# Quarter-tile weights in layer 3 and a re-searched instruction order for a four-layer graph network

## The chip, the core and the metric

The kernel runs on one NeuronCore of a Trainium2 chip. The metric is the device time of one launch in microseconds; lower is better. The five engines of the core run their own instruction streams, each strictly in its own order, and wait for one another by semaphores: TensorE (PE: matrix products, with the weight loads PEld beside them), VectorE (DVE), ScalarE (ACT), GpSimd (POOL) and SyncE (SP, which here only issues DMAs).

## What is computed

There are 16 independent graphs, each with 1024 nodes of 256 features and a 1024 x 1024 adjacency matrix of zeros and ones. Four layers follow one another, each as "normalise, relu, graph layer, add to x":

```
h = relu(layernorm(x));  x = x + relu(h @ W_upd + mean over neighbours of (h @ W_msg) + bias)     # layer 0
h = relu(layernorm(x));  x = x + layernorm_per_head(relu(attention(h)) + h @ W)                   # layer 1: 4 heads of 64
h = relu(layernorm(x));  x = x + elu(attention(h))                                                # layer 2: 4 heads of 64
h = relu(layernorm(x));  x = x + attention(h)                                                     # layer 3: 1 head of 256
```

In the attentions the score of a pair of nodes is `leaky_relu(e_src[i] + e_dst[j])`, pairs without an edge are left out, a softmax is taken over j, and the result weighs the rows of `h @ W`.

## The kernel before

**The factored attention.** A softmax weight is `exp(leaky_relu(s + t))`. It is the larger of two products, each of a factor of i and a factor of j. After a factor of i has been divided out (a softmax allows it), the unnormalised weight of the pair is `max(r[i], tt[j]) * mask[j, i]`, and the remaining factor of j, `exp(t)`, is multiplied into the rows of `h @ W`. `terms` makes the factors: `es = exp((1 - slope) * s)` is transposed, goes to DRAM (`rd`, through SP) and comes back broadcast to all partitions (`r`, one DMA per head in `spread`); `tt = exp(-(1 - slope) * t)` stays in SBUF. `bounds` (lines 1050 to 1052) notes the extremes of t and s. At the end of the launch they are compared with `TERM_MAX`, and a general kernel, which is not entered with these inputs, would be taken if they were too large.

**The weights and the products.** `masked` (line 1083) is one VectorE `scalar_tensor_tensor`: for a block jb of 128 nodes it writes the weights for `hi - lo` nodes i into a tile `p` of 128 x 1024. In layers 1 and 2 it writes all 1024 columns, and the product of that block (line 1266, called "head product" below) is 16 small matrix products with 65 columns that go to alternate 64-wide halves of the array. Each of the 4 heads has 8 such blocks. In layer 3 one operation writes only 256 columns, and the product (line 1420) is two matrix products of 257 columns; there are 4 x 8 of them per graph. The tag `p` has six buffers of 128 x 1024, and each call of `masked` takes a new one, in layer 3 too. `terms` also takes one of them for `r4`, and so do the weight matrices at the start.

**The other work.** `norm_t` makes the layer norm (VectorE statistics, GpSimd's root, ScalarE's `hn`, TensorE's transposes at line 967, ScalarE's copy to `ht`). `project` (line 984) is `h @ W`. Layer 0 gathers with eight blocks of adjacency columns (`adjr`, three buffers, loaded on GpSimd's queue, lines 1143 and 1146); its masks for the later layers come from a second load of the adjacency (`nat`, on SP's queue), squared on ScalarE and transposed by DMA. The epilogues of the heads run on VectorE, ScalarE and GpSimd.

**What sets the order.** All instructions are recorded with `Plan.do`, each with its engine, a cost in microseconds written out by hand, what it reads and writes, and a priority: the position of its graph (`plan.pos`, which grows by the TensorE costs), plus a slack, plus the `RANK` of its stage and engine. `Plan.emit` then does list scheduling over all 16 graphs: at each step it takes the instruction that can start first by the costs and, where these are equal, the one of lowest priority value. The order in which it takes them is the order of the instructions on each engine; on the chip only this order and the semaphores remain. Graph b starts at position `b * SHIFT`, with `SHIFT` 38.75, and a gate holds graph b + 2 back until layer 3 of graph b has begun.

Of the kernel before, what the change touches and what calls it, by code (L numbers as in the profile page):

```python
# [25 lines left out]

SHIFT = 38.75

ENGINES = ("pe", "dve", "act", "pool", "sp")
RANK = {  # L30
    "load": (-255, -45, -146, -223, -161),
    "setup": (147, 44, -129, 45, 72),
    "norm0": (132, -159, -111, 18, -3),
    "split0": (-94, 119, -51, -165, -111),
    "mask": (77, 143, 41, 193, 218),
    "gather0": (241, -7, 71, 23, 10),
    "norm1": (-60, -62, -162, -146, -99),
    "project1": (20, 26, -5, 26, -6),
    "weights1": (-164, 7, -45, 57, -13),
    "heads1": (-192, -212, -213, -62, -111),  # L40
    "last1": (-26, -102, 9, -196, -80),
    "norm2": (-206, -157, 81, 6, -21),
    "project2": (79, -60, -360, 87, -40),
    "weights2": (94, -3, 153, -153, 12),
    "heads2": (-112, -33, -288, -105, -59),
    "last2": (-21, -230, -230, -36, -82),
    "norm3": (-477, -373, -518, -355, -261),
    "project3": (148, 162, -14, -78, 0),
    "weights3": (170, 143, 167, 44, 87),
    "last3": (43, -259, -75, -14, -59),  # L50
}
BUFS = {
    "x": 3, "ht": 2, "wide": 6, "mask": 3, "adjr": 3, "nat": 2, "sq": 2,
    "hn": 2, "r": 3, "p": 6, "o": 2, "t": 2, "y": 2, "rd": 4,
    "mv": 4, "st": 2, "rstd": 4, "shift": 4, "tt": 3, "es": 2, "dg": 2, "rden": 2, "sth": 1, "mh": 2, "rsh": 2,
    "acc": 2, "mm": 4,
# [15 lines left out]
class Plan:  # L72
# [8 lines left out]
    def __init__(self):  # L81
        self.ops, self.pos, self.gate, self.stage = [], 0.0, None, None

    def do(self, eng, cost, fn, r=(), w=(), lag=0.0, slack=0.0, kind="f", dma=0.0):

        k, deps = len(self.ops), set() if self.gate is None else {self.gate}
        for keys, writes in ((r, False), (w, True)):
            for key in keys:  # L90
                buf, part = key if isinstance(key, tuple) else (key, None)
                parts = [part, None] if part is not None else list(set(buf.last) | set(buf.readers) | {None})
                for q in parts:
                    if q in buf.last:
                        deps.add(buf.last[q])
                    if writes:
                        deps.update(buf.readers.get(q, ()))
                buf.users.append(k)
        for key in r:
            buf, part = key if isinstance(key, tuple) else (key, None)  # L100
            buf.readers.setdefault(part, []).append(k)
        for key in w:
            buf, part = key if isinstance(key, tuple) else (key, None)
            if part is None:
                buf.last, buf.readers = {}, {}
            buf.last[part] = k
            buf.readers[part] = []
        bufs = list(dict.fromkeys(key[0] if isinstance(key, tuple) else key for key in (*r, *w)))
        deps.discard(k)
        self.ops.append((eng, cost, lag, fn, deps, bufs, self.pos + slack + RANK[self.stage][ENGINES.index(eng)], kind, dma))  # L110
        if eng == "pe":
            self.pos += cost

    def emit(self):
# [6 lines left out]
        done, free, held = [None] * n, {}, {}  # L121
        kept, moved = "f", 0.0

# [5 lines left out]
        while ready:  # L129
            best = None  # L130
            for k in ready:
                eng, cost, lag, fn, deps, bufs, prio, kind, dma = self.ops[k]
                at = free.get(eng, 0.0)
# [7 lines left out]
                for buf in bufs:  # L141
                    if buf.t is None:
# [3 lines left out]
                        if len(ends) >= m:  # L146
# [3 lines left out]
                            at = max(at, ends[m - 1] + 0.1)  # L150
                if at is not None and (best is None or (at, prio, k) < best):
                    best = (at, prio, k)
            at, _, k = best
            eng, cost, lag, fn, deps, bufs, _, kind, dma = self.ops[k]
            for buf in bufs:
# [443 lines left out]
def tile_factored(  # L599
# [55 lines left out]
    deg = const.tile([P, B * NB], F32, name="f_deg")  # L655
    mx = const.tile([P, B * 9], F32, name="f_mx")
    rdn = const.tile([P, B * NB], F32, name="f_rdn")

# [249 lines left out]
    def norm_t(xs, by_block=False):  # L908
# [3 lines left out]
        for hf in range(2):  # L912
# [34 lines left out]
            for i2 in range(2):  # L947
# [20 lines left out]

                do("pe", 0.46, turn, r=[hn], w=[pt])
                i0 = (hf * nh + 2 * i2) * P  # L970
# [7 lines left out]
    def project(ps, ht, ib, w, lo, hi, k=0):  # L978


        def go():
            out = ps.t[:, : hi - lo] if hi - lo > D else ps.t[:, k, :]
            for c in range(KC):
                nc.tensor.matmul(  # L984
                    out,
                    ht.t[:, c, ib * P : (ib + 1) * P],
                    w.t[:, c, lo:hi],
                    start=(c == 0 and k == 0),
                    stop=(c == KC - 1),
                    skip_group_check=k > 0,  # L990
                )

        do("pe", 0.88, go, r=[(ht, ib // 2), w], w=[ps])

# [14 lines left out]
    def terms(wh, nh, slope, ecol, scol, k):  # L1009


        tt = buf(small, "tt", [P, NB, nh])
        r4 = buf(work, "p", [P, N])
        rd = buf(dram, "rd", [nh, N])

        def ed():
            return wh.t[:, :, ecol::E1][:, :, :nh] if nh > 1 else wh.t[:, :, ecol : ecol + 1]

        m = NB * nh
        es = buf(small, "es", [P, nh, NB])  # L1020
        do(
            "act",
            0.25,
            lambda: nc.scalar.activation(
                es.t, wh.t[:, :, scol : scol + nh].rearrange("p n h -> p h n"), AF.Exp, scale=1.0 - slope
            ),
            r=[(wh, ib) for ib in range(NB)],
            w=[es],
        )
# [3 lines left out]
            0.11,  # L1033
            lambda: nc.tensor.transpose(pt.t[:m, :P], es.t.rearrange("p h n -> p (h n)"), ident),
            r=[es],
            w=[pt],
# [10 lines left out]

        def bounds():
            es = wh.t[:, :, scol : scol + nh]
            nc.vector.tensor_reduce(mx[:, k : k + 1], ed(), AX.XY, ALU.max)  # L1050
            nc.vector.tensor_reduce(mx[:, k + 1 : k + 2], ed(), AX.XY, ALU.min, negate=True)
            nc.vector.tensor_reduce(mx[:, k + 2 : k + 3], es, AX.XY, ALU.max)

        do("dve", 0.4, bounds, r=[wh])

        def raise_t():
            nc.scalar.activation(tt.t, ed(), AF.Exp, scale=-(1.0 - slope))
            nc.scalar.activation(ed(), ed(), AF.Exp)

        do("act", 0.5, raise_t, w=[tt, wh])  # L1060

# [12 lines left out]

        return tt, spread

    def masked(r, tt, mask, jb, h, lo, hi):

        w = buf(work, "p", [P, N])
        do(  # L1080
            "dve",
            (hi - lo + 125) / 960.0,
            lambda: nc.vector.scalar_tensor_tensor(  # L1083
                w.t[:, : hi - lo], r.t[:, lo:hi], tt.t[:, jb, h : h + 1], mask.t[:, jb, lo:hi], op0=ALU.max, op1=ALU.mult
            ),
            r=[r, tt, mask],
            w=[w],
        )
        return w
# [143 lines left out]
    def heads(b, l, xs, mask, w, slope, epilogue, keep):  # L1233
# [19 lines left out]
        for h in range(H):  # L1253
# [5 lines left out]
            for jb in range(NB):  # L1259
# [13 lines left out]

                do("pe", 0.94, product, r=[p, xw], w=[ps], kind="c")
            plan.stage = f"heads{l}" if h + 1 < H else f"last{l}"
            epilogue(b, h, ps, wh, xs, 8.0 if h + 1 < H else 0.0)

# [18 lines left out]
    def epilogue1(b, h, ps, wh, xs, slack):  # L1296
# [44 lines left out]

        do("pool", 2.0, root, r=[mb], w=[rs], lag=0.9, slack=slack)
        do(
# [52 lines left out]
    def layer3(b, xs, mask):  # L1396
# [15 lines left out]
        for i2 in range(NB // 2):  # L1412
            plan.stage = "weights3"
            ps = buf(acc_p, "acc", [P, 2, 512])
            for jb in range(NB):
                w = masked(r, tt, mask, jb, 0, i2 * 2 * P, (i2 + 1) * 2 * P)

                def product(w=w, ps=ps, jb=jb):
                    for q in range(2):
                        nc.tensor.matmul(  # L1420
                            ps.t[:, q, : D + 1],
                            w.t[:, q * P : (q + 1) * P],
                            wh.t[:, jb, : D + 1],
                            start=(jb == 0),
                            stop=(jb == NB - 1),
                        )

                do("pe", 0.87, product, r=[w, (wh, jb)], w=[ps])
            k = b * NB + 2 * i2
# [11 lines left out]
            for q in range(2):  # L1441
                do(
                    "dve",
                    0.5,
                    lambda q=q, i2=i2, ps=ps, o=o, k=k: nc.vector.scalar_tensor_tensor(  # L1445
# [25 lines left out]
    for b in range(B):  # L1471
        plan.pos, plan.gate = b * SHIFT, gates.get(b)
        xs, adjr = load_x(b) if b else first, {k: load_adjr(b, k) for k in range(2)}
# [15 lines left out]
    nc.vector.tensor_reduce(tot, ps[:, : B * NB].rearrange("p (b n) -> p b n", n=NB), AX.X, ALU.add)  # L1489
    for k, (t, most) in enumerate(((tot, 0.0), (mx, TERM_MAX), (rdn, 1e30))):  # L1490
        nc.vector.tensor_scalar(t, t, most, None, op0=ALU.is_le)
        nc.vector.tensor_reduce(m[:, k : k + 1], t, AX.X, ALU.min)
# [58 lines left out]
```

## Time and profile before

| what | us |
|---|---|
| three runs, median (lowest, highest) | 2740.07 (2736.87, 2740.48) |
| the profiled execution | 2741.27 |
| its span, first to last instruction | 2739.4 |
| mean granted TensorE clock in it | 0.972 |
| VectorE, weights of 1024 columns (line 1083), 1024 of them | 1251.0 busy, 1276 ns each |
| VectorE, weights of 256 columns (line 1083), 512 of them | 222.4 busy, 477 ns each |
| TensorE, head products (line 1266), 1024 of 16 | 1064.6 busy |
| TensorE, layer-3 products (line 1420), 512 of 2 | 462.2 busy |

A row of the costliest groups has the line, the engine and the operation, the tiles as out<-in, the count, the busy time, the mean duration of one, and the idle time of the engine just before, with what ended it. Matrix products are pipelined, so the duration of one is longer than the distance from one start to the next, and each product of 32-bit numbers stands as two instructions in the trace (32 per head product, 4 per layer-3 product). "Granted clock" is the share of the full TensorE clock that was allowed in a stretch.

### The profile page before, as it was taken

What the parts mean: (1) busy time and instruction counts of PE and PEld (TensorE: products, weight loads), DVE (VectorE), ACT (ScalarE), POOL (GpSimd) and SP (SyncE); (2) the same over time, 40 slices, a digit from 0 to 9 for tenths busy, and PEclk for the clock granted to TensorE, in tenths of its full rate; (3) what the DMA queues carried; (4) which work ended last, traced back from release to release, by engine and by line L of the source; (5) the groups of instructions that cost most, each with busy time, mean ns of one, the idle gap of its engine ahead of it and who ended that gap; (6) DMA issues with size and microseconds to landing.
All of it is one profiled execution on the core that took longest, in us unless ns stands there. A gap on an engine that the chain in (4) does not pass through costs nothing. (4 is left out here: it accounts for less than half of the span.)

```text
span 2739.4 us, 92386 instructions
## 1 busy us (share of the span) xinstructions
PE 2547.4 (93%) x40667; PEld 2285.7 (83%) x40667; DVE 2357.3 (86%) x4790; ACT 1143.5 (42%) x2753; POOL 878.0 (32%) x907
## 2 busy tenths in 40 slices
PE   7867999999999999999999999999999999999786
PEld 6767798888888888889888889888888988888775
DVE  2699689898988989899898989989898898989884
ACT  4431625344353444525344452534435353453222
POOL 3332234324252332424224251422425133241210
PEclk9989999999999999999999999999999999999998
DMA  8724547356472745547255563735546263562121
GB/s 194 171 44 84 113 87 165 82 128 117 99 143 53 159 91 129 105 91 163 60 144 97 118 125 71 163 75 133 112 107 134 63 158 81 130 118 66 33 52 29
DMA packets 397318, 293.58 MB, mean 107 GB/s; under 512 B 179301, under 2 KB 345706, under 8 KB 396906
## 3 DMA queue, kind: packets, MB, share of 16 engines
q0 software_dynamic: 232992, 92.29, 24.8%
q1 hardware_dynamic: 160752, 193.05, 24.4%
q8 instruction: 321, 5.26, 0.8%
q10 hardware_dynamic: 3162, 2.24, 0.3%
q14 instruction: 91, 0.75, 0.1%
HBM read 228.21 MB, written 17.37 MB: 90 GB/s over the span
## 5 line engine op out<-in xcount | busy, mean ns | idle before, releaser
L1083 DVE SCALAR_TENSOR_TENSOR p<-r,tt,mask 128x1024 f32<-128x1024 f32 (+1 forms) x1536 | 1473.3, 1010 | 109.2 <-PE acc L1266 40.8
L1266 PE MATMUL acc<-wide,p 128*64 128x65 f32 x32768 | 1064.6, 227 | 135.7 <-DVE p L1083 129.3
L1266 PEld LDWEIGHTS acc<-wide,p 128*64 128x64 f32 x32768 | 1017.2, 141 | 204.0 <-issue 99.0
L984 PE MATMUL mm<-f_w,ht 128*128 128x264 f32 (+2 forms) x2048 | 477.0, 387 | 1.4 <-ACT ht L973 1.3
L1420 PE MATMUL acc<-wide,p 128*128 128x257 f32 x2048 | 462.2, 382 | 10.1 <-DVE p L1083 9.9
L1420 PEld LDWEIGHTS acc<-wide,p 128*128 128x128 f32 x2048 | 386.1, 191 | 68.1 <-issue 11.1
L984 PEld LDWEIGHTS mm<-f_w,ht 128*128 128x128 f32 x2048 | 384.6, 192 | 61.2 <-ACT ht L973 3.0
L954 ACT ACTIVATE hn<-x,shift,rstd 128x256 f32<-128x256 f32 x512 | 269.1, 591 | 257.5 <-DVE shift L941 157.1
L1356 ACT ACTIVATE t<-t,mh,rsh 128x64 f32<-128x64 f32 x512 | 176.7, 428 | 198.2 <-DVE mh L1346 174.3
L1143 PE MATMUL mm<-wide,adjr 128*128 128x258 f32 x1024 | 254.5, 289 | 0.0
L1146 PE MATMUL mm<-wide,adjr 128*128 128x256 f32 x1024 | 247.9, 282 | 0.0
L1003 ACT COPY wide<-mm 128x264 f32<-128x264 f32 (+1 forms) x384 | 141.3, 378 | 218.7 <-PE mm L984 216.5
L1216 POOL DMA_DIRECT2D x<-y x48 | 76.6, 1596 | 447.4 <-DVE y L1388 435.8
L934 POOL TENSOR_SCALAR rstd<-mv 128x4 f32<-128x4 f32 x128 | 60.7, 474 | 434.6 <-DVE mv L929 402.3
L1143 PEld LDWEIGHTS mm<-wide,adjr 128*128 128x128 f32 x1024 | 195.9, 191 | 1.7
L1146 PEld LDWEIGHTS mm<-wide,adjr 128*128 128x128 f32 x1024 | 194.2, 190 | 1.5
L922 DVE BATCH_NORM_STATS2 st<-x 128x6 f32<-128x256 f32 x512 | 183.2, 412 | 8.4 <-DMA x<-in_x_dram 5.6
L967 PE MATMUL mm<-f_ident,hn 128*128 128x128 f32 x1024 | 168.0, 300 | 20.2 <-ACT hn L954 17.2
L973 ACT COPY ht<-mm 128x512 f32<-128x512 f32 x256 | 137.8, 580 | 104.9 <-PE mm L967 103.9
L1157 POOL TENSOR_SCALAR dg<-f_deg 128x1 f32<-128x1 f32 x128 | 61.0, 476 | 359.7 <-ACT f_deg L1154 357.4
L967 PEld LDWEIGHTS mm<-f_ident,hn 128*128 128x128 f32 x1024 | 125.2, 151 | 50.4 <-ACT hn L954 35.5
L935 POOL TENSOR_TENSOR rstd<-rstd,f_mhalf 128x4 f32<-128x4 f32 x128 | 162.2, 1268 | 10.7
(103 smaller groups left out, 2179.3 us busy)
## 6 DMA issues: line engine op xcount, KB each, us to landing
r<-rd SPq DMA_DIRECT2D x144, 512.0 KB, 3.9
adjr<-in_adj_dram POOLq DMA_DIRECT2D x128, 512.0 KB, 4.7
nat<-in_adj_dram SPq DMA_DIRECT2D x128, 512.0 KB, 6.6
out_dram<-o SPq DMA_DIRECT2D x64, 256.0 KB, 2.8
x<-in_x_dram SPq DMA_DIRECT2D x31, 512.0 KB, 5.1
x<-t POOLq DMA_DIRECT2D x48, 256.0 KB, 5.5
x<-y POOLq DMA_DIRECT2D x48, 256.0 KB, 4.5
mask<-sq SPq DMA_TRANSPOSE x128, 4.7
```

What stands on the lines that cost most here:

```text
L922: lambda st=st, ib=ib, k=k: nc.vector.bn_stats(st.t[:, k, :], xs.t[:, ib, :]),
L935: nc.gpsimd.tensor_tensor(rstd.t, rstd.t, mhalf[:, :nh], op=ALU.pow)
L954: nc.scalar.activation(hn.t[:, k, :], xs.t[:, hf * nh + q, :], AF.Relu, bias=shift.t[:, q : q + 1], scale=rstd.t[:, q : q + 1],)
L967: nc.tensor.transpose(pt.t[:, k, c, :], hn.t[:, k, c * P : (c + 1) * P], ident)
L984: nc.tensor.matmul(out, ht.t[:, c, ib * P : (ib + 1) * P], w.t[:, c, lo:hi], start=(c == 0 and k == 0), stop=(c == KC - 1), skip_group_che ...
L1003: lambda ib=ib, ps=ps: nc.scalar.copy(wh.t[:, ib, :cols], ps.t[:, :cols]),
L1083: lambda: nc.vector.scalar_tensor_tensor(w.t[:, : hi - lo], r.t[:, lo:hi], tt.t[:, jb, h : h + 1], mask.t[:, jb, lo:hi], op0=ALU.max, op1= ...
L1143: nc.tensor.matmul(ps.t[:, : D + 2], a.t[:, ib, :], hi.t[:, ib, : D + 2], start=(ib == 0), stop=False)
L1146: nc.tensor.matmul(ps.t[:, :D], a.t[:, ib, :], lo.t[:, ib, :D], start=False, stop=(ib == NB - 1))
L1266: nc.tensor.matmul(ps.t[c : c + 64, g, q * E1 : (q + 1) * E1], p.t[:, i2 * 64 : (i2 + 1) * 64], xw.t[:, jb, h * E1 : (h + 1) * E1], start= ...
L1356: nc.scalar.activation(t.t[:, ib, :], t.t[:, ib, :], AF.Identity, bias=mb.t[:, 3, ib : ib + 1], scale=rs.t[:, ib : ib + 1],)
L1420: nc.tensor.matmul(ps.t[:, q, : D + 1], w.t[:, q * P : (q + 1) * P], wh.t[:, jb, : D + 1], start=(jb == 0), stop=(jb == NB - 1),)
```

## The change

Layer 3's weights share a tile: four calls of `masked` fill the four quarters of one `p`, and each product reads its own quarter. `r4` moves out of `p` into a tag of its own with one buffer of 128 x 128. `tt` and `es` become the two halves of one tile `et`, and the check of the terms' size reads the exponentials instead of their arguments (two reductions instead of three, against limits `f_lim` which six memsets write at the start).

`Plan` gets three rules. Operations that carry a `row` (all calls of `masked` within a graph) must follow each other in the order in which they were recorded. An operation whose start lies within `HOLD` of the earliest on the same engine may go before it if its priority value is lower. A count of weights made and not yet used (`stock`) could favour weights below `LOW`; with `FIRST = 0` it does nothing. `SHIFT` becomes 193.25, each graph gets an offset `START`, the `RANK` table and the slacks of the epilogues get new numbers, and some costs change (transposes 0.46 to 0.5, projections 0.88 to 0.89, head products 0.94 to 0.955, layer-3 products 0.87 to 0.875, GpSimd's head root 2.0 to 2.6).

```diff
-SHIFT = 38.75
+SHIFT = 193.25
+LOW, FIRST = 5, 0
+HOLD = (0.1, 0.2, 0.1, 0.0, 0.0)
+START = (83, 357, 209, 320, 312, 341, 221, 275, 166, 245, 168, 116, 90, 156, 43, -288)
 RANK = {
...
-    "weights2": (94, -3, 153, -153, 12),
-    "heads2": (-112, -33, -288, -105, -59),
+    "weights2": (-26, 73, 114, -256, 21),
+    "heads2": (-318, -725, -739, -720, -508),
...
-    "mv": 4, "st": 2, "rstd": 4, "shift": 4, "tt": 3, "es": 2, "dg": 2, "rden": 2, "sth": 1, "mh": 2, "rsh": 2,
+    "mv": 4, "st": 2, "rstd": 4, "shift": 4, "et": 3, "r4": 1, "dg": 2, "rden": 2, "sth": 1, "mh": 2, "rsh": 2,
...
+        if row is not None:
+            if row in self.rows:
+                deps.add(self.rows[row])
+            self.rows[row] = k
...
-                if at is not None and (best is None or (at, prio, k) < best):
-                    best = (at, prio, k)
-            at, _, k = best
...
+                if at is not None:
+                    could.append((at, prio, k))
+                    if best is None or could[-1] < best:
+                        best = could[-1]
+            at, prio, k = best
+            until = at + HOLD[ENGINES.index(self.ops[k][0])]
+            for a, p, q in could:
+                if self.ops[q][0] == self.ops[k][0] and a <= until and p < prio:
+                    at, prio, k = a, p, q
...
-        r4 = buf(work, "p", [P, N])
+        r4 = buf(small, "r4", [P, P])
...
-            nc.vector.tensor_reduce(mx[:, k : k + 1], ed(), AX.XY, ALU.max)
-            nc.vector.tensor_reduce(mx[:, k + 1 : k + 2], ed(), AX.XY, ALU.min, negate=True)
-            nc.vector.tensor_reduce(mx[:, k + 2 : k + 3], es, AX.XY, ALU.max)
...
+            nc.vector.tensor_reduce(mx[:, k : k + 2], et.t.rearrange("p s h n -> p s (h n)"), AX.X, ALU.max)
+            nc.vector.tensor_reduce(mx[:, k + 2 : k + 3], ed(), AX.XY, ALU.max)
...
-    def masked(r, tt, mask, jb, h, lo, hi):
+    def masked(r, tt, mask, jb, h, lo, hi, w=None, q=0):
...
-        w = buf(work, "p", [P, N])
+        w = w or buf(work, "p", [P, N])
+        c = q * (hi - lo)
...
-                w.t[:, : hi - lo], r.t[:, lo:hi], tt.t[:, jb, h : h + 1], mask.t[:, jb, lo:hi], op0=ALU.max, op1=ALU.mult
+                w.t[:, c : c + hi - lo],
+                r.t[:, lo:hi],
+                tt.t[:, 1, h, jb : jb + 1],
+                mask.t[:, jb, lo:hi],
+                op0=ALU.max,
+                op1=ALU.mult,
             ),
-            r=[r, tt, mask],
-            w=[w],
+            r=[r, (tt, 1), mask],
+            w=[(w, q)],
+            row="weights",
+            stock=1,
...
-                w = masked(r, tt, mask, jb, 0, i2 * 2 * P, (i2 + 1) * 2 * P)
-
-                def product(w=w, ps=ps, jb=jb):
-                    for q in range(2):
+                q = jb % 4
+                w = masked(r, tt, mask, jb, 0, i2 * 2 * P, (i2 + 1) * 2 * P, w if q else None, q)
+
+                def product(w=w, ps=ps, jb=jb, q=q):
+                    for k in range(2):
+                        c = (2 * q + k) * P
...
-        plan.pos, plan.gate = b * SHIFT, gates.get(b)
+        plan.rows = {}
+        plan.pos, plan.gate = b * SHIFT + START[b], gates.get(b)
```

## The prediction

> **What bounds the kernel now.** I read the page first, then the busy time by 90 us windows, the waits, the timeline around one wait, and the order in which the two built programs hold their instructions.
>
> ```profile
> PE 2547.4 (93%) x40667; PEld 2285.7 (83%) x40667; DVE 2357.3 (86%) x4790; ACT 1143.5 (42%) x2753; POOL 878.0 (32%) x907
> ...
> PE   7867999999999999999999999999999999999786
> ```
>
> ```profile
> 180.00:270.00 90.00, 69.57 (x1661) 64.06 (x1659) 87.66 (x146) 24.60 (x62) 25.60 (x16) 0.87 0.34 70
> ...
> 810.00:900.00 90.00, 89.33 (x1324) 79.50 (x1324) 79.58 (x145) 29.85 (x73) 22.54 (x25) 1.00 0.33 66
> 900.00:990.00 90.00, 84.46 (x1310) 75.15 (x1309) 83.11 (x205) 51.09 (x124) 44.10 (x46) 0.98 0.72 153
> ...
> 2610.00:2700.00 90.00, 71.06 (x1180) 60.71 (x1179) 58.53 (x93) 26.09 (x60) 7.26 (x7) 0.92 0.21 46
> ```
>
> The columns are busy PE, PEld, DVE, ACT and POOL, granted clock, DMA share and GB/s. TensorE sets the time, with VectorE close behind it, and the loss has three places: the first 290 us, a repeated dip in the middle, and the last 220 us.
>
> ```profile
> PE acc L1266 <- DVE p L1083: 129.3, 56, 8.5
> ...
> DVE p L1083 <- PE acc L1420: 35.3, 79, 4.9
> ```
>
> TensorE waits for VectorE's weights 129.3 us in all, and elsewhere VectorE waits, 79 times, for layer 3's products to give a buffer back. The two are one event, seen around 900 us on TensorE and then on VectorE:
>
> ```profile
> 895.81 5.37 PE L1420 MATMUL acc<-wide,p 128*128 128x257 f32 x24
> 905.31 1.67 PE L1266 MATMUL acc<-wide,p 128*64 128x65 f32 x32 [4.14 <-DVE p L1083]
> ```
>
> ```profile
> 896.66 1.66 DVE L1083 SCALAR_TENSOR_TENSOR p<-r,tt,mask 128x256 f32<-128x256 f32 x4
> 898.24 0.68 DVE L1388 SCALAR_TENSOR_TENSOR y<-y,t 128x512 f32<-128x512 f32 x1
> 898.96 0.69 DVE L1227 TENSOR_TENSOR x<-x,y 128x512 f32<-128x512 f32 x1
> 899.68 1.40 DVE L922 BATCH_NORM_STATS2 st<-x 128x6 f32<-128x256 f32 x4
> ...
> 903.89 2.47 DVE L1083 SCALAR_TENSOR_TENSOR p<-r,tt,mask 128x1024 f32<-128x1024 f32 x2
> ```
>
> Each layer-3 weight takes a whole one of the six buffers `p`, though it fills a quarter. So TensorE has six products in hand (24 instructions, 5.37 us), while VectorE is away from weights for 5.6 us (898.24 to 903.89) and then needs 1.2 us more. The wait comes in every graph. What follows it is in the windows of TensorE alone:
>
> ```profile
> 901.20:905.30 4.10, 0.00 (x0) 1.00 0.42 124
> 905.70:909.10 3.40, 3.40 (x41) 0.51 1.20 292
> ```
>
> After 4.1 us idle, 3.4 us run at half clock (6.8 us in other graphs).
>
> **The ledger of before,** against this execution's own span of 2739.4 us (2741.3 with what lies around it; the median of the runs is 2740.1). Work at the start-to-start distance of undisturbed rows: 1024 head products at 0.944 us, 512 layer-3 products at 0.868, 512 projections at 0.876, 128 gathers at 1.90, 256 groups of four transposes at 0.436, 64 updates at 2.17, and 23 us of small ones: 2377 us. The order holds 176 excursions out of head products into other work and back. Eight in a row take 7.69 us and nine 8.62, so 0.93 each and 0.25 for the way in and out; start-to-start it is 0.12 and 0.09. With the gathers' changes this is 46 us. Total 2423; the other 316 is loss. In the middle a graph takes 162.3 us (eleven recurrences of this wait, 581.1 to 2366.4) for 151.3 us of work and changes. Its loss of 11.0 is 5.2 waits (4.13, 0.58, 0.51), 2.6 half clock, and 3.2 small delays. By 290 us the loss is about 94, and 71 come in the tail.
>
> **Part 1: quarter tiles and the order, middle.** Six buffers now hold 24 layer-3 weights, 21 us of products instead of 5. VectorE's work is unchanged (512 operations of 128x256, 0.396 us start to start). I laid VectorE's instructions between a released buffer and the next needed weight against TensorE's work between the same two points, with these row durations. In before this gives a deficit of 4.2 us per graph (trace: 4.1 and 0.6 over the same stretch); in after the worst stretch of a graph is 1.3 to 2.1. I take 2.3, and 0.5 for ScalarE as now: the waits fall from 5.2 to 2.8, a gain of 2.4. If the cover fails (another chain, say `rsh` on GpSimd, holds VectorE), it is 5.2 again.
>
> A rule bears on what the shorter waits do to the clock. The row: 4.1 us idle, then 3.4 to 6.8 at half rate; between 2644 and 2669 us six waits of 0.6 to 0.9 cost no clock. The Trainium skill ("TensorE: Matmul & The Clock Gate", Part 1) says that the clock halves after at least one idle window of about 3.4 us. By the rule all 2.6 us per graph go; by the row I keep 0.6 for bad alignment: gain 2.0.
>
> **Part 2: more changes of kind.** The new order breaks the products up to keep VectorE abreast: runs of 8 head products become runs of 2 to 5, and the excursions go from 176 to 326. At 0.21, with the gathers' changes, that is 83 us instead of 46: +37, of which 2.4 per graph. The skill speaks against exactly this: "TensorEngine Tiling (Array Packing)", Key Properties, says that a change of tiling mode drains the array, and head products write 64-wide tiles among 128-wide work. It names no price; at the 0.25 of the rows above, modelled ends included, the extra would be about 44. I take 37, because the start-to-start distance is what the next instruction sees. Middle: -2.4 -2.0 +2.4 = -2.0 per graph, over 13.4 graphs **-27**.
>
> **Part 3: the start.** In before the first products stand behind 83 us of TensorE work, in which two graphs are mixed, and start at 111.5. With DMA 94% busy in the first 90 us, graph 1's loads are ahead of what graph 0 needs. In after, 67 us stand ahead, all eight of graph 0's gathers come before any of graph 1's, and its adjacency loads come first on both SP's and GpSimd's queue. Until its last gather graph 0 needs some 11.8 MB (two graphs' `x`, the weight matrices, the adjacency for `adjr` and `nat`), 60 us at the 196 GB/s of the first window. I put the eighth gather at 64 us (75.5 now) and the first product at 95. From there VectorE sets the pace: before its last large start wait VectorE has 200 us of work ahead in before, 155 in after for 166 of TensorE's. With 79 us idle instead of 87, TensorE is 68 us late instead of 94: **-26**. Bounds: nothing, if the DMA is no earlier; -40, if the weights start at 80.
>
> **Part 4: the tail.** In before TensorE ends with graph 15 alone:
>
> ```profile
> 2681.88 3.14 PE L967 MATMUL mm<-f_ident,hn 128*128 128x128 f32 x12 [7.80 <-ACT hn L954]
> ...
> 2701.28 29.59 PE L1420 MATMUL acc<-wide,p 128*128 128x257 f32 x128 [6.27 <-DVE p L1083]
> ```
>
> These two waits and the half clock that follows (10.2 and 6.8 us at 0.5) make 22 us. In after, eight of graph 14's layer-3 products stand in the first gap, and twelve more around graph 15's `es` transpose, ahead of its own first product: 7 and 10 us of work for gaps of 7.8 and 6.3. The earlier tail, where VectorE is short (deficit 29 in either order), stays. **-22.** Changes of kind in the start and tail: **+5**.
>
> **Part 5: edits with one answer.** `bounds` reads exponentials in two reductions instead of three: VectorE -0.1 us, 48 times, under TensorE's work. It is due later; now VectorE stands 111 us behind ScalarE there, and in after some 3 us per graph remain, in time that VectorE has. `r4` leaves the six `p` and gets one buffer, wanted three times in 160 us: nothing. Six memsets on GpSimd before the first load: +0.2 us. `START`, `HOLD`, the per-graph order of weights and the costs act only through the order.
>
> **Sum:** 2740 - 27 - 26 - 22 + 5 = **2670 us**.
>
> **Rivals.** (a) *The changes of kind are paid and the waits come back.* My deficits follow VectorE and TensorE only. The new order puts `shift` and `mh` a few quarter weights behind GpSimd's roots (0.9 and 2.3 us), and VectorE queues behind them. If that brings over 5 us of waits per graph, with their half clock, the middle loses 2.4 x 13.4 = 32 and start and tail gain nothing: 2740 + 37 = **2777**. The point is a wait of about 5 us per graph. Against it: VectorE has 15 us to spare per graph (162.3 against 2357.3/16). 12%. (b) *Only the middle works:* the start is held by DMA and the tail by its chain: 2740 - 27 + 5, about **2718**. For it: DMA at 0.94. 18%. (c) *The small delays of 3.2 us go with the waits,* since they sit in the windows of low clock: 2.4 x 13.4 further, **2638**. 17%. (d) *The same time:* gains and changes of kind cancel, 4%.
>
> **Numbers.** My forecast 49%, the rest as above. From 2632 to 2728 leaves about 2 in 10 outside. A measurement of this kernel can't tell less than 0.2% (5.5 us) from no change: faster 84%, same 4%, slower 12%.
>
> **What would show it.** Right: no 4 us wait at a layer's start in the middle, hardly any half-clock window between 400 and 2400 us, a graph in about 160 us, the first product near 95 us, PE's last gap before layer 3 filled. Wrong: a wait of 4 us per graph elsewhere, a graph over 162 us, the first product still after 105 us.

## The result, and the profile after

The changed kernel takes **2757.4 us** (median of four runs, 2752.0 to 2759.2) against 2740.3 for the kernel before, measured beside it (2736.9 to 2742.7): a ratio of 1.006, 95% interval 1.0042 to 1.0078. It is slower by 0.6%, where 2670 was forecast. Its profiled execution took 2752.0 us, with a span of 2750.1 and a mean granted clock of 0.984 (before: 2739.4 and 0.972).

First the page of the changed kernel: busy time and instructions by engine, and TensorE's busy tenths in 40 slices.

```profile
PE 2587.8 (94%) x40667; PEld 2262.6 (82%) x40667; DVE 2350.8 (85%) x4742; ACT 1143.3 (42%) x2753; POOL 852.9 (31%) x913
...
PE   7878999999999999999999999999999999998788
```

The same 40667 TensorE instructions are busy for 40 us more (2547.4 before), although the clock is higher. Against this TensorE stands idle for 162 us instead of 192. The waits of TensorE (total us, times, longest) show that the wait of before has gone from its place:

```profile
PE acc L1297 <- DVE p L1107: 49.8, 51, 5.4
PE acc L1297 <- DVE o L1478: 21.5, 6, 6.2
PE mm L992 <- ACT hn L979: 18.3, 4, 13.2
PE acc L1297 <- DVE t L1317: 17.0, 19, 2.4
```

The waits for weights fell from 129.3 to 49.8 us. Two of these rows are new, those of `o` and of `t`. In both TensorE has a weight in hand, and waits for VectorE's epilogue to read out one of the two `acc` buffers. One such event, in TensorE's timeline (start, length, instruction, idle time before it and its releaser) and then in VectorE's:

```profile
1545.19 9.80 PE L1453 MATMUL acc<-wide,p 128*128 128x257 f32 x44
1559.15 3.74 PE L1297 MATMUL acc<-wide,p 128*64 128x65 f32 x64 [4.16 <-DVE o L1478]
```

```profile
1552.14 1.28 DVE L1107 SCALAR_TENSOR_TENSOR p<-r,et,mask 128x1024 f32<-128x1024 f32 x1 [4.57 <-issue]
...
1554.78 1.41 DVE L947 BATCH_NORM_STATS2 st<-x 128x6 f32<-128x256 f32 x4
...
1558.12 0.88 DVE L1478 SCALAR_TENSOR_TENSOR o<-acc,f_rdn,x 128x256 f32<-128x256 f32 x2
```

The quarter tiles do what they were forecast to do: eleven layer-3 products run in a row. But then VectorE, which stood 4.57 us for a reason that the profile doesn't name, and has a weight, an epilogue and two rounds of statistics ahead of `o` in its queue, gives `acc` back some 4 us late.

**The ledger.** Up to the start of the last TensorE instruction, the time is split as in the prediction: waits (idle time before instructions), half clock (half the length of the windows with a granted clock of 0.5), work (instructions times the start-to-start distance of undisturbed ones), and the rest, which is what changes of kind cost and stalls too short to show as idle time. The experiments are added for later reading; "excursions" are read from the order of the instructions. Idle time within half-clock windows (34 us before, 20 in the changed kernel) counts in full as a wait and by half as half clock, so the rest comes out too small; the last column has it with this time counted once.

| kernel | waits | half clock | work | rest | end | excursions | rest, idle once |
|---|---|---|---|---|---|---|---|
| before | 186 | 78 | 2380 | 89 | 2733 | 176 | 106 |
| changed | 156 | 46 | 2380 | 162 | 2744 | 326 | 171 |
| before, cheap weights | 140 | 68 | 2380 | 53 | 2640 | 176 | 66 |
| changed, cheap weights | 117 | 31 | 2380 | 127 | 2656 | 326 | 133 |
| before, wide head products | 121 | 290 | 3243 | -10 | 3644 | 176 | 8 |
| changed, wide head products | 64 | 159 | 3243 | 10 | 3476 | 326 | 19 |
| quarter tiles only | 327 | 119 | 2380 | 94 | 2920 | 145 | 132 |
| price raised in the list | 330 | 121 | 2380 | 120 | 2951 | 119 | 149 |
| changed, reordered | 119 | 22 | 2380 | 145 | 2666 | 282 | 150 |
| before, reordered | 193 | 71 | 2380 | 83 | 2727 | 196 | 99 |
| changed, reordered, old price | 121 | 35 | 2380 | 143 | 2679 | 351 | 152 |
| changed, reordered longer | 124 | 29 | 2380 | 134 | 2667 | 263 | 138 |

The changed kernel saves 30 us of waits and 32 of half clock and loses 73 in the rest: 11 us, the difference of the spans. I had charged 37 for the last and 107 as gain for the first two. So of the 81 us between forecast (-70) and ledger (+11), 45 are gains that fell short and 36 are the rest.

Where the rest comes from can be read in the two traces. I took each TensorE instruction's distance from the one before it, less idle time, half clock and the undisturbed distance. The first instruction after a change out of or back to head products and the two behind it are late by 43 us in all before, and by 100 in the changed kernel: 57 of the 66 us of the last column. But the rest is no count of excursions alone: with the price raised in the list it is 149 us at 119 excursions, and there the short stalls within runs are some 90 us, for some 40 in the changed kernel.

### The profile page after: what moved, and what is told of

Same layout as the page of the kernel before. It is cut to its first block, busy times and chain, and to the rows that moved or that the text cites. A ratio compares the mean times of both kernels' runs of the same rounds, so it can differ in the third digit from the quotient of the medians.

```text
span 2750.1 us, 92338 instructions
## 1 busy us (share of the span) xinstructions
PE 2587.8 (94%) x40667; PEld 2262.6 (82%) x40667; DVE 2350.8 (85%) x4742; ACT 1143.3 (42%) x2753; POOL 852.9 (31%) x913
## 4 chain that ended last, share of the span: by engine, by line
PE 58%; DVE 26%; DMA 6%; issue 5%; POOL 3%; ACT 2%; SPq 0%; ACTq 0%; DVEq 0%; POOLq 0%
PE acc L1297 21%; DVE p L1107 13%; PE mm L1009 11%; PE acc L1453 10%; PE mm L1213 4%; PE mm L1174 4%; PE mm L1177 4%; DMA r<-rd 3%; DVE st L947 2%; PE mm L992 2%; DMA mask<-sq 2%; DVE t L1317 2%; DVE sth L1360 2%; POOL rstd L960 1%; DVE t L1349 1%
## 5 line engine op out<-in xcount | busy, mean ns | idle before, releaser
L1107 DVE SCALAR_TENSOR_TENSOR p<-r,et,mask 128x1024 f32<-128x1024 f32 (+1 forms) x1536 | 1466.1, 1010 | 77.3 <-DMA r<-rd 35.7
L1297 PE MATMUL acc<-wide,p 128*64 128x65 f32 x32768 | 1087.9, 226 | 108.1 <-DVE p L1107 49.8
L1009 PE MATMUL mm<-f_w,ht 128*128 128x264 f32 (+2 forms) x2048 | 500.7, 391 | 1.6 <-ACT ht L998 1.6
L1453 PE MATMUL acc<-wide,p 128*128 128x257 f32 x2048 | 485.5, 384 | 5.9 <-DVE p L1107 2.0
L1009 PEld LDWEIGHTS mm<-f_w,ht 128*128 128x128 f32 x2048 | 376.1, 191 | 65.6 <-ACT ht L998 8.1
L1453 PEld LDWEIGHTS acc<-wide,p 128*128 128x128 f32 x2048 | 379.0, 190 | 60.2 <-issue 7.5
L992 PE MATMUL mm<-f_ident,hn 128*128 128x128 f32 x1024 | 157.2, 287 | 19.7 <-ACT hn L979 18.3
L904 POOL DMA_DIRECT2D adjr<-in_adj_dram x128 | 128.2, 1072 | 94.0 <-PE mm L1177 90.8
L992 PEld LDWEIGHTS mm<-f_ident,hn 128*128 128x128 f32 x1024 | 117.8, 144 | 46.5 <-ACT hn L979 26.2
```

What stands on the lines that cost most here:

```text
L992: nc.tensor.transpose(pt.t[:, k, c, :], hn.t[:, k, c * P : (c + 1) * P], ident)
L1009: nc.tensor.matmul(out, ht.t[:, c, ib * P : (ib + 1) * P], w.t[:, c, lo:hi], start=(c == 0 and k == 0), stop=(c == KC - 1), skip_group_che ...
L1107: lambda: nc.vector.scalar_tensor_tensor(w.t[:, c : c + hi - lo], r.t[:, lo:hi], tt.t[:, 1, h, jb : jb + 1], mask.t[:, jb, lo:hi], op0=ALU ...
L1297: nc.tensor.matmul(ps.t[c : c + 64, g, q * E1 : (q + 1) * E1], p.t[:, i2 * 64 : (i2 + 1) * 64], xw.t[:, jb, h * E1 : (h + 1) * E1], start= ...
L1453: nc.tensor.matmul(ps.t[:, k, : D + 1], w.t[:, c : c + P], wh.t[:, jb, : D + 1], start=(jb == 0), stop=(jb == NB - 1),)
```

## The experiments

Theory: an excursion out of the head products and back costs about 0.37 us, not 0.21, because the next instruction but one is late too. Rivals: the price is right and VectorE's waits, in its own queue order, eat the gain; or the quarter tiles are good and the new order spoils them.

**1. The price alone.** Stages of TensorE products on operands in SBUF, with equal work and a different number of excursions:

```diff
+    stages = (
+        (head, acc, 8, project, mm, 4, 1), (head, acc, 2, project, mm, 1, 4),
+        (head, acc, 8, last, ac2, 4, 1), (head, acc, 2, last, ac2, 1, 4),
+        (wide, acc, 8, project, mm, 4, 1), (wide, acc, 2, project, mm, 1, 4),
+    )
```

> Nothing of the stack is computed: six stages of TensorE products alone, on operands that are in SBUF. Stages 1 and 2 hold the same 80 head products and 40 projections, with 10 excursions out of the head products and with 40; stages 3 and 4 the same with 40 layer-3 products instead of projections; stages 5 and 6 as 1 and 2, with the head product as eight matmuls 128 columns wide instead of sixteen of 64. Theory (an excursion costs 0.37 us: 0.12 to leave, 0.10 at the second instruction of the entered run, 0.09 to come back, 0.05 at the third head matmul): stage 2 is 30 x 0.37 = 11 us longer than stage 1, stage 4 as much longer than stage 3, stage 6 within 1 us of stage 5. Rival (my prediction's 0.21 us, the rest being waits for VectorE): 6.3 us and 6.3 us. Rival (the cost is of any change of operand, not of the tile's width): stage 6 is also 6 to 11 us longer than stage 5.

TensorE's timeline in the first stage, then in the second:

```profile
29.71 7.69 PE L51 MATMUL acc<-wh,p 128*64 128x65 f32 x256
37.32 3.83 PE L72 MATMUL mm<-w,ht 128*128 128x264 f32 x16
41.08 7.69 PE L51 MATMUL acc<-wh,p 128*64 128x65 f32 x256
...
201.38 2.09 PE L51 MATMUL acc<-wh,p 128*64 128x65 f32 x64
203.40 1.16 PE L72 MATMUL mm<-w,ht 128*128 128x264 f32 x4
204.48 2.09 PE L51 MATMUL acc<-wh,p 128*64 128x65 f32 x64
```

Starts are compared, not lengths. Eight head products and four projections take 41.08 - 29.71 = 11.37 us; two and one take 3.10, and four times that is 12.41. Three more excursions cost 1.04 us, **0.346 each**. With layer-3 products the medians are 11.28 and 3.08: 0.347. With wide head products they are 17.853 and 4.463: 0.000. The theory holds. Another operand or another output alone costs nothing here; the cost belongs to the change between 64-wide and 128-wide tiles (whether to the width or to leaving the alternation of the two halves, these stages don't part).

**2. No reading of the exponentials.** The two reductions of `bounds` are left out (their target `mx` is set to zero once at the start):

```diff
-            nc.vector.tensor_reduce(mx[:, k : k + 2], et.t.rearrange("p s h n -> p s (h n)"), AX.X, ALU.max)
-            nc.vector.tensor_reduce(mx[:, k + 2 : k + 3], ed(), AX.XY, ALU.max)
+            pass
```

> Changed kernel without the two reductions over ScalarE's exponentials (48 x 2 VectorE instructions; the check value of the bounds is not computed), same order of everything else. Rival (VectorE's wait for ScalarE there, 6.4 us per graph, ahead of weights in its queue, makes TensorE's new waits): 30 us or more faster than the changed kernel, about 2725. Theory (the price of the excursions carries the loss; this wait lies in time that VectorE has): within 10 us of the changed kernel, 2747 to 2757.

Measured: 2755.7 us, ratio to before 1.0056 (1.0043 to 1.0069), so the same as the changed kernel. In the changed kernel VectorE waits 99.8 us for those exponentials. Here, in VectorE's waits and then in TensorE's:

```profile
DVE wide L1278 <- ACT wide L1075: 124.2, 18, 13.9
```

```profile
PE acc L1297 <- DVE p L1107: 48.3, 52, 5.4
PE acc L1297 <- DVE o L1478: 20.5, 6, 6.2
```

VectorE's wait is taken over by the next instruction that needs ScalarE: its row was 21.4 us, which with the 99.8 makes 121. TensorE's waits stay. So the two reductions cost nothing where they stand. What VectorE's wait for ScalarE itself costs, this run can't tell, because the wait did not go away; it is 6.4 us per graph in the middle (70.2 us over eleven graphs) where the prediction had 3.

**3. Wide head products,** in the changed kernel and in the one before, same order. The head product writes the same values with eight matrix products of 128 columns:

```diff
-                    for i2 in range(2 * NB):
-                        g, q = divmod(i2 // 2, 4)
-                        c = i2 % 2 * 64
+                    for i2 in range(NB):
+                        g, q = divmod(i2, 4)
...
-                            ps.t[c : c + 64, g, q * E1 : (q + 1) * E1],
-                            p.t[:, i2 * 64 : (i2 + 1) * 64],
+                            ps.t[:, g, q * E1 : (q + 1) * E1],
+                            p.t[:, i2 * P : (i2 + 1) * P],
```

> Changed kernel, same order, the head product as eight matmuls of 128 columns instead of sixteen of 64, so that no excursion changes the tile's width. If a wide product takes the same 0.94 us: theory (0.37 us per excursion, 326 of them) takes up to 120 us out of TensorE's work, of which VectorE (2357 us busy) lets some half show: 2650 to 2700. Rival (0.21 us): at most 68 us out, 2690 to 2730. Rival (stalls behind VectorE's order are what the change lost by): 2740 or more.

> Kernel before, same order, with the same wide head products. Theory (0.37 us, 176 excursions): at most 65 us less, 2685 to 2715, and slower than the wide changed kernel by 20 us or more, since with the price gone the quarter tiles' gain stands alone. Rival (0.21 us): at most 37 less, 2705 to 2730. Rival (the order's stalls carry the loss): the wide changed kernel is again no faster than this one.

Measured: 3504 and 3650 us, ratios to before 1.280 and 1.330. The forecasts of both totals rested on a wide product that takes the same 0.94 us, and it takes 1.79 (first experiment), so the totals answer nothing. The ledger does. The rest now differs by 20 us between the two orders instead of by 73 (by 10 instead of 66 with idle time counted once): without changes of width, 53 to 56 us of the difference are gone, which is 150 excursions at 0.35 to 0.37. What stays I put down to the other changes of kind, those into and out of the gathers and the products that prepare them (the "fp32r split"). The new order has 107 more of them (185 for 78), but no run tries them alone. And the changed kernel is now the faster one, by 168 us in the profiled executions (146 by the medians): 57 less in waits and 131 in half clock, 20 more in the rest. Most of this is half clock, which wide products keep for long stretches (last section), so its size says little of quarter tiles. TensorE's wait for weights in the kernel before with wide products, then in the changed one, where it comes second to 17.6 us for `hn`:

```profile
PE acc L1265 <- DVE p L1083: 81.7, 21, 6.9
```

```profile
PE acc L1296 <- DVE p L1107: 12.1, 6, 4.2
```

**4. Cheap weights,** in both kernels, same orders:

```diff
-                w.t[:, : hi - lo], r.t[:, lo:hi], tt.t[:, jb, h : h + 1], mask.t[:, jb, lo:hi], op0=ALU.max, op1=ALU.mult
+            lambda: nc.vector.tensor_copy(w.t[:, : hi - lo], r.t[:, lo:hi]),
```

> Kernel before, same order on every engine, each attention weight made by a plain copy of r instead of the maximum times the mask (the mask and the exponentials are not applied), so that VectorE's largest operation takes about half as long and its work falls from 2357 to some 1700 us. TensorE's 192 us of waits and most of its half clock then have no cause but the start, the tail and other engines: all theories expect 2500 to 2600 here. It is the base for the next run.

> Changed kernel, same order, the same cheap weights. Theory (the order's 150 more excursions cost 0.35 us each whatever VectorE does): slower than the kernel before with cheap weights by 30 to 55 us, the 52 us of excursions less what the earlier start of graph 0 saves. Rival (the loss is new waits behind VectorE's order, which now has slack): no slower, or faster by up to 20 us.

Measured: 2647.3 and 2669.8 us (ratios 0.9647 and 0.9735). VectorE falls to 1730 us of work in the first and 1723 in the second, and the new order is still 22 us slower. The base did not come down to the 2500 to 2600 us that I expected: TensorE waits 140 us in it, for 186 before, and most of that is still for weights, though they are cheap:

```profile
PE acc L1264 <- DVE p L1083: 86.0, 25, 7.8
```

So two thirds of the 129.3 us stay when a weight of 1024 columns takes 713 ns for 1276. In the pages of the two (busy time by engine):

```profile
PE 2500.8 (94%) x40667; PEld 2272.3 (86%) x40667; DVE 1729.8 (65%) x4790; ACT 1141.8 (43%) x2753; POOL 802.8 (30%) x907
```

```profile
PE 2538.5 (95%) x40667; PEld 2239.4 (84%) x40667; DVE 1722.6 (65%) x4742; ACT 1137.9 (43%) x2753; POOL 784.5 (29%) x913
```

The rival falls: with a VectorE that has slack the rest differs by 74 us, as with the full weights (67 and 66 with idle time counted once). The result lies below the 30 to 55 that the theory gave, since I left out that the quarter tiles still save 22 us of waits and 37 of half clock here.

**5. Quarter tiles alone, and the price told to the list.** The first is the kernel before with the four quarters in one `p` and nothing else; the second changes one line of the changed kernel:

```diff
-    EMPTY = {"cf": 0.12, "cr": 0.12, "fc": 0.09, "fr": 0.09, "rc": 0.09, "rf": 0.19}
+    EMPTY = {"cf": 0.23, "cr": 0.23, "fc": 0.14, "fr": 0.09, "rc": 0.14, "rf": 0.19}
```

> Kernel before with layer 3's weights in quarter tiles and nothing else (old ranks, old costs, no order of the weights, no hold). By its instruction order it has 145 excursions (176 before, 326 in the changed kernel), and VectorE's work between a freed buffer and the next needed weight exceeds TensorE's between the same points by 197 us in all (128 before, 73 changed). Theory (both excursions and deficits count, each at its measured price): 31 x 0.35 = 11 us less and up to 69 us more wait: 2760 to 2810, slower than the changed kernel. Rival (the quarter tiles alone remove the 4 us wait of each graph, and the new order is what spoils it): 2670 to 2720.

> Changed kernel, its planner told the measured prices of a change of kind (0.23 us out of the head products, 0.14 back, for 0.12 and 0.09), same ranks. It then orders 119 excursions instead of 326, and the deficits by the instruction order rise from 73 to 298 us. Theory (an excursion is worth 0.35 us, a deficit its own length): 207 x 0.35 = 72 us less and up to 225 us more: 2820 to 2910. Rival (waits by the instruction order are hidden, excursions alone cost): 2690.

Measured: 2928.8 (1.0684) and 2961.6 us (1.0798, two runs). Both rivals fall, and the theory's sizes with them. Few excursions are no merit in themselves: the waits rise to 327 and 330 us. The deficits that I count from VectorE's and TensorE's order alone do not match these rises: 69 us for 141 in the first case (against the kernel before), 225 for 174 in the second (against the changed one). In the first TensorE waits for ScalarE too. The list of TensorE's waits with quarter tiles only has

```profile
PE acc L1267 <- DVE p L1084: 170.5, 92, 8.8
PE mm L967 <- ACT hn L954: 62.2, 16, 12.2
```

where the second row was 17.2 us before. In both cases a table of ranks that was found for one set of buffers and costs did not carry over to another.

**6. The order searched with the right price.** The list is used as a model of the whole program: with its costs and rules, but with 0.23 and 0.12 us for the change of kind, it tells when a given order would end. From the changed kernel's order, instructions of one engine are moved past each other as long as that end comes earlier; the order found is stored in the kernel.

```diff
-        ready = [k for k in range(n) if not left[k]]
-        while ready:
...
+        steps = array.array("h", zlib.decompress(base64.b85decode(ORDER)))
+        for k in itertools.accumulate(steps):
+            fn, bufs = self.ops[k][3], self.ops[k][5]
             for buf in bufs:
                 if buf.t is None:
                     buf.t = buf.make()
...
             fn()
```

> Changed kernel with the same instructions, buffers and quarter tiles, its order on each engine searched once more from the present one: instructions of one engine are moved past each other as long as the list's own model of the whole program, told the measured prices of a change of kind (0.23 us out of the head products, 0.12 back), gets shorter. 282 excursions instead of 326, 38 runs of the fp32r split instead of 61. The model gives 2706 us for the changed kernel's order, 2693 for the one before, 2630 for this; chip minus model is 51 and 47 us for the two that were measured. Theory (with the price right, the model ranks orders as the chip does, and the changed kernel lost by the price that its list was told): about 2680, at most 2705, faster than both kernels. Rival (what the changed kernel lost lies in waits that the list doesn't hold, so that the model says nothing): 2740 or more.

> Kernel before (whole tiles for layer 3), its order searched in the same way for the same time: 196 excursions, model 2653 us for 2693. Theory: about 2700, that is slower than the reordered quarter tiles by 10 to 40 us, because the model still holds 168 us of TensorE waits here against 76 there, which quarter tiles make possible. Rival (quarter tiles bring nothing once both orders are priced rightly): equal to the other within 5 us, or faster.

Measured: **2673.3 us** for the changed kernel reordered (ratio 0.9747, 0.9732 to 0.9762), and 2730.0 for the kernel before (0.9951, 0.9934 to 0.9968). The first beats both kernels: 2.5% under the one before, 3.1% under the changed one (0.9747 / 1.006). Its waits of TensorE, and the window from 245 to 2505 us (TensorE's, its loads', VectorE's, ScalarE's and GpSimd's busy time, granted clock, DMA share, GB/s):

```profile
PE acc L1400 <- DVE p L1210: 48.8, 56, 5.6
...
PE acc L1400 <- DVE t L1420: 4.7, 11, 1.3
```

```profile
245.00:2505.00 2260.00, 2201.05 (x35603) 1945.32 (x35601) 2041.14 (x4151) 986.69 (x2418) 770.27 (x788) 1.00 0.57 112
```

The wait for `o` is gone from the largest rows and the one for `t` has shrunk from 17.0 to 4.7 us: neither was forced by the buffers, only by the order. No window at half clock is left between 244 and 2506 us. Against the changed kernel the ledger has 37 us less waits, 24 less half clock, and 17 less rest, where 44 fewer excursions at 0.346 are 15. The kernel before gains less than forecast (2700): the model holds 168 us of waits for its order, the chip has 193, and 186 in before. So whole tiles cost 57 us once both orders are searched alike, for 10 to 40 forecast; the two kernels also differ in the smaller edits (`r4`, `bounds`, costs), and each had one search.

**7. The same search at the old price, and a longer one.** The price in the model is set back to 0.12 and 0.09; the other run goes on from the reordered kernel.

> The reordered quarter tiles once more, the same search from the same start, for the same time and with the same seed, but with the price of a change of kind out of and back to the head products as the changed kernel's list has it (0.12 and 0.09 us, my prediction's 0.21). It ends with 351 excursions where the search at the measured price ended with 282. By the old price this order is 12 us better than that one (2610 against 2622), by the measured price 37 us worse (2667 against 2630). Theory (0.35 us): about 2710, 25 to 45 us slower than the reordered kernel at 2673. Rival (0.21 us): about 2660, faster than it.

> The reordered quarter tiles, searched for 25 minutes more at the measured price: 263 excursions, model 2618 us (2630 for the reordered kernel, which took 2673). Theory: chip minus model stays at 43 to 51, about 2661 to 2668, the fastest of all. Rival (the model is at its end as a guide): equal to the reordered kernel within 4 us.

Measured: 2687.1 us (0.9801, 0.9783 to 0.9818) and 2676.5 us (0.9767, 0.9751 to 0.9784). The order found at the old price is 14 us slower, not faster: the sign is the theory's, the size about half. Its 69 more excursions cost TensorE 17 us in the gaps between instructions of different kinds and at the two that follow them, but 15 us of short stalls within runs went away in exchange, which the model doesn't hold; 13 us of half clock make the difference. The longer search gained nothing, where the model promised 12: here the rival was right. Chip less model is 51 us for the changed kernel and 47 for the one before, then 43, 77, 20 and 58 for the four searched orders as they stand in the ledger: so even differences of some 30 us are beyond this model.

The old price also bears on what experiment 6 shows. The search with that price, and with more excursions than the changed kernel (351 for 326), still takes 70 us off it (2757 to 2687). Only 14 of the 84 us that the reordered kernel gains go with the price. The others come from searching the order on a model of the whole program, and they lie in the waits (156 to 121), the half clock (46 to 35) and the rest (162 to 143). That the changed kernel lost because its list was told the wrong price is therefore not shown; that its order pays for the excursions is.

## Why the prediction was wrong

**The step that failed first is Part 2's price, "at 0.21".** It took the distance from the last head product to the first foreign instruction, and from the last foreign one back (0.12 and 0.09), and called this "what the next instruction sees". The second instruction after a change is late as well: 0.10 us in projections and layer-3 products, 0.05 at the third matrix product of a head product. Alone it is 0.346 us, so 150 excursions cost 52 us and not 31.5. The other changes of kind were miscounted too: at the list's own prices (0.09 into a gather or split, 0.19 out of it) all changes come to 46 us before, as stated, but to 91 and not 83 in the changed kernel, so 14 us more for the others and not 5.5. The two together make 66; +37 was +73, or 66 with idle time counted once. The two rows of 7.69 and 8.62 us, from which I had 0.25 as the upper bound, couldn't show it: they end with the head products, and their ends are modelled. The Trainium skill's rule ("TensorEngine Tiling (Array Packing)", Key Properties) that a change of tiling mode drains the array was right to speak against the change, and the 0.346 us fit it, though no run shows the draining itself; the price had to be measured, by the second start and not by the first.

The list holds the same 0.12 and 0.09. With each kernel's own costs `emit` ends the two orders at 2668 and 2666 us; told the measured price, the model has 2693 and 2706 (experiment 6), and so the changed kernel behind, as on the chip. What this did to the search for its ranks can only be judged by experiment 7: there the old price cost 14 us.

**Part 1, waits -2.4 and clock -2.0 per graph, is the second step that failed:** -0.75 and -1.5 (5.69 to 4.94, 2.64 to 1.14; 13 half-clock windows between 400 and 2400 us before, 6 after). The 4 us wait at the layer's start did vanish, and VectorE does keep abreast. What I did not follow is the way back: with twenty-four weights in hand TensorE often stands until VectorE's epilogues free `acc`. TensorE's waits over eleven graphs of the middle, in before (581.2 to 2366.5 us) and then in the changed kernel (581.5 to 2402.4):

```profile
PE acc L1266 <- DVE p L1083: 55.6, 23, 4.1
```

```profile
PE acc L1297 <- DVE o L1478: 13.4, 4, 4.2
PE acc L1297 <- DVE t L1317: 13.1, 16, 2.4
PE acc L1297 <- issue: 9.4, 11, 1.6
PE acc L1297 <- DVE p L1107: 8.0, 23, 1.1
```

The wait for weights fell by 48 us, and 26 came back as waits for `o` and `t`. So the cover failed by another chain than the `rsh` that I had named; a wait of about 4 us, my sign of error, stands in two of the eleven graphs, not in each. The clock halved after shorter waits than the window of about 3.4 us in Part 1's rule, too: after waits of 2.94, 2.37 and 2.41 us (ending at 731.1, 1229.9 and 1720.2 us). Rival (a) gave the right sign by a cause that did not occur: waits did not come back to over 5 us more per graph, they fell a little.

**In sum,** a graph took 165.3 us in the middle, for 162.3 before and 160 forecast, which is past the limit of 162 that I had set: -0.75 for waits, -1.5 for the clock, +5.25 for the rest, where I had -2.4, -2.0 and +2.4. With idle time counted once the rest rose by 5.1: 3.9 at the changes out of and back to head products, and 1.2 elsewhere, where I had put nothing. By place, counting how far TensorE lags behind its own work at 400 us, at 2500 us and at the end, the start gave -13, the middle +40 (-27 forecast) and the tail -16.

**Part 3, the start, -26:** the first head product came at 93.7 us (95 forecast), but by 270 us TensorE was 84 us late, not 68, because it then waited five times for 3 to 5 us. **Part 4, the tail, -22:** -16, with its changes of kind. Neither was tried by itself; in the reordered kernel both are part of the whole. **Part 5** holds as far as it was tried: the reductions cost nothing (experiment 2).

## What to carry to other kernels

Measure the price of a switch by the whole detour, out and back, in a run that does nothing else: distances between neighbours miss what the second instruction pays. Give it to the scheduler before searching, since a search spends freely whatever is priced too low (351 excursions for 282 here, and 14 us). Search the order on a model of the whole program: here that was worth more than the right price. And judge a larger stock of operands by the whole ring that it feeds: when the input wait goes, the wait for output buffers may be next.

## What was not expected of the hardware

A 32-bit matrix product of 65 columns with a 128-column weight block takes 0.223 us (1.787 us for eight), and two with 64-column blocks in alternate halves of the array take 0.118 (0.944 for sixteen). The columns alone don't set the pace of the wide product: a projection's instruction of 264 columns takes 0.222 us, so one of 65 should take some 0.055 (an estimate from that row), but they stand 0.112 apart. The weights' loads of these products are listed as busy for 293.7 us and the products for 291.3, so I take the load to set the pace and the halves to overlap it; no run tries this.

With those wide products TensorE can stay at half clock for long, though it hardly rests. In the kernel before with wide products, one window (TensorE busy first, granted clock third from the end):

```profile
277.30:441.10 163.80, 159.44 (x747) 159.25 (x747) 75.12 (x109) 13.59 (x30) 22.45 (x16) 0.50 0.22 44
```

The clock falls during a wait of 3.6 us and stays at 0.50 for 164 us, with TensorE listed as busy for 159 of them. The instructions stand 0.213 us apart in this window, for 0.112 at full clock, so the slow clock is real. In the first experiment the same products, with projections among them, ran at 1.00 for 357 us, having started there. Why the clock does not recover was not tried.
